# Two graph layers on sparse lists: variances and score sums on ScalarE, Newton steps and column copies in another iteration, five pair sums in a tile

## The chip, the cores and the metric

The kernel runs on one core of one Trainium2 chip. The metric is device time in microseconds (us) of one execution. The kernel before took 1013.26 us (median of three runs, 1010.72 to 1016.06); the execution that was profiled took 1008.23 us, of which its trace spans 1006.5 us.

In the text PE or TensorE is the matmul engine, DVE is VectorE, ACT is ScalarE, POOL is GpSimd and SP is SyncE, which here only issues transfers.

## The reference, cut to what matters

A graph of N = 3327 nodes with 512 features each passes through two layers, each with a residual and a layer norm. The adjacency matrix has a handful of ones in a row.

```python
# layer 0: graph attention with 4 heads of 128
feats  = einsum('nf,hfo->hno', x, W)
logits = leaky_relu(e_s[:, :, None] + e_n[:, None, :], 0.2) + NEG_INF * (1 - adj)
out    = relu(softmax(logits) @ feats + b)            # heads side by side: 512
x      = layernorm(x + out)
# layer 1: one attention over neighbours and one plain sum, each with a gate
attn_a = sigmoid([adj @ x, x] @ Wa.T + ba)
attn_b = sigmoid([adj @ x, x] @ Wb.T + bb)
h      = x @ W_sa
e      = where(adj != 0, exp(-leaky_relu(s_left[:, None] + s_right[None, :], 0.01)), 0)
x_a    = (e / (e.sum(1) + 1e-5)) @ h
x_b    = adj @ (x @ W_gcnb) + b_gcnb
x      = layernorm(x + sigmoid(attn_a * x_a + attn_b * x_b))
```

The layer norm is (y - mean) / sqrt(variance + 1e-5) over the 512 features.

## The kernel before, in words

The function `sparse_pass` does the work in three stages. Nodes lie in 26 tiles of 128. Every engine runs its own instructions in the order in which the program gives them (a manual schedule); engines wait for each other by semaphores.

**Preparation.** The adjacency matrix comes in seven chunks of 512 columns, through 12 buffers. For each chunk TensorE turns it into codes (`make_codes`), VectorE takes from them the list of each node's neighbours (`top_codes`, `decode`, `pick`). Between the chunks `features` computes one tile of layer 0's features after another on TensorE (L346), ScalarE copies them into a row (L350 to L352), and GpSimd writes the rows to `table0` in DRAM (L353). Behind the last tile one more small write, of `nrow` (L355), sets the scores of the padding row to -1e30. Nodes are sorted by their number of neighbours, in two groups of 12 and 14 tiles: `rank_a`, `rank_b` and `sort` write the lists of group 0 in the order of rank during chunk 4 and those of group 1 after the last chunk. `own_x` then gathers group 0's own rows of x. The first tile of each group (tiles 0 and 12) has nodes with more neighbours than a tile has slots; the rest are in an extra row of gathers, the stairs. `climb(g)` moves the numbers and scores of these from the sorted list onto the right partitions, with one matmul (L538) and small copies of VectorE. `climb(0)` runs in the loop over chunks, at chunk 4 (`i == NC0 + 1`, with NC0 = 3).

**Layer 0.** The tiles come in an order of their own, `order0` (11, 10, 0 to 9, 12 to 25), and have as many rows to sum as neighbours: 16 for tile 0, down to 5 for tile 25. In iteration i, GpSimd issues the gathers for tile i + 3 (L602, one instruction a row of 128 x 520 floats, into seven buffers of six rows), and:

- `weigh_a` and `weigh_b` compute the softmax weights of tile i + 1: scores (L696), their maximum, Exp on ScalarE (L709), sum, reciprocal and product (L714 to L716);
- `attend` multiplies every gathered row by its weight, two thirds of the rows on VectorE (L733), every third on ScalarE (L731), and TensorE adds them up in PSUM by matmuls with the identity (L736), behind one for the bias (L725);
- for tile i - 1, VectorE adds x (L810, `scalar_tensor_tensor`, called STT in places), and `columns1` transposes the result on TensorE (`x1t`, L753); `stats` takes mean and variance with bn_stats (L647, L648);
- for tile i - 2, `columns2` copies the transposed tile to SBUF on ScalarE (`xt`, L757) and multiplies it with eight vectors (`pcol`, L760), from which layer 1 gets its scores and gates; `columns3` copies these (L764).

Variances are gathered in groups of up to four tiles (`Norm`). At the end of a group, `rsqrt` computes 1/sqrt with an integer start and three Newton steps on VectorE (L656 to L663, 13 small instructions), and two iterations later `publish` scales the group's tiles (ScalarE, L768), corrects the eight columns (VectorE, L771 and L772) and scatters each tile's rows to `table1` (GpSimd, L143).

**Layer 1** starts when all rows of `table1` are written. Tiles come in `order`: six short ones, then long and short in turn, last three of 9, 9 and 7 rows. In iteration i:

- `weights_a` and `weights_b` compute the attention weights and gates of tile i + 1: a copy on ScalarE (L861), the sums of scores on VectorE, one for each gather buffer (L863), leaky ReLU (L870), Exp on ScalarE with an accumulated sum (L872), gates (L874 to L887), L892 to L895;
- `scaled_first` starts the weighted sum `sw` on ScalarE (L914), and `weighted` adds the rows to it on VectorE, one STT each (L930);
- the plain sum of the same rows is made by TensorE, one matmul with the identity a row (L951). To spare matmuls, VectorE adds some rows two and two (L932): `paired` chooses up to four pairs in a tile, five where there are 13 rows or more. Part 0 of `weighted` goes up to the last pair, part 1 is what is left;
- `turn` and `project` transpose both sums and multiply them with two matrices of 512 x 512 (L961, L963, L970), for tile i - 1;
- for tile i - 2 follow the gated sum (L995), Tanh on ScalarE (L997), the residual (L1018), bn_stats and, at the end of a group, the Newton steps; an iteration later ScalarE scales the group (L1011) and GpSimd scatters it to the output.

Of the kernel before, what the change touches and what calls it, by code (L numbers as in the profile page):

```python
# [14 lines left out]
P = 128  # L15
# [64 lines left out]
def sparse_pass(  # L80
# [213 lines left out]
    nrow = pj.tile([1, ROW], F32, name="nrow")  # L294
    nc.gpsimd.memset(nrow, 0.0)
    nc.gpsimd.memset(nrow[:, F : F + H], -BIG)
# [42 lines left out]
    def features(t):  # L339
# [11 lines left out]
        nc.scalar.copy(row[:, F:ROW].rearrange("p (h o) -> p h o", h=2), pf[:, :, F // 2 : HC])  # L351
        nc.scalar.copy(st[:, t, S + 2 : S + 2 + H].bitcast(F32), pf[:, 1, F // 2 : HC])  # L352
        nc.gpsimd.dma_start(table0[t * P : (t + 1) * P, :], row)  # L353
        if t == NT - 1:
            nc.gpsimd.dma_start(table0[N:NP, F : F + H], nrow[:, F : F + H])  # L355
# [194 lines left out]
    for i in range(len(chunks)):  # L550
# [11 lines left out]
        if i == NC0 + 1:  # L562
            climb(0, p0, psl.tile([P, CH], F32, tag="pc1", name="climb0")[:, : B + H])
# [3 lines left out]
    nc.sync.dma_start(own1[:, 1, :], table0[NG[0] * P : NP, :])  # L567
    rank_a(1)
# [76 lines left out]
    def stats(pool, y, mv):  # L645
        st6 = pool.tile([P, 6], F32, tag="st6", name=f"st6_{nc.next_id()}")
        nc.vector.bn_stats(st6, y)  # L647
        nc.vector.bn_aggr(mv, st6)  # L648

    def rsqrt(pool, mv, n, tag):  # L650

        v = pool.tile([P, GRP], F32, tag="rv", name=f"rv{tag}")[:, :n]
        r = pool.tile([P, GRP], F32, tag="rr", name=f"rr{tag}")[:, :n]
        t = pool.tile([P, GRP], F32, tag="rt", name=f"rt{tag}")[:, :n]
        d = pool.tile([P, GRP], F32, tag="rd", name=f"rd{tag}")[:, :n]
        nc.vector.tensor_scalar(v, mv[:, :n, 1], LN_EPS, None, ALU.add)  # L656
        nc.vector.tensor_scalar(t.bitcast(I32), v.bitcast(I32), 1, None, ALU.logical_shift_right)
        nc.vector.tensor_scalar(r.bitcast(I32), t.bitcast(I32), -1.0, float(0x5F3759DF), ALU.mult, ALU.add)
        for _ in range(3):
            nc.vector.tensor_mul(t, r, r)  # L660
            nc.vector.scalar_tensor_tensor(t, t, -0.5, v, ALU.mult, ALU.mult)
            nc.vector.scalar_tensor_tensor(r, t, 1.5, r, ALU.add, ALU.mult)
        nc.vector.scalar_tensor_tensor(d, mv[:, :n, 0], -1.0, r, ALU.mult, ALU.mult)  # L663
        return r, d

    class Norm:


        def __init__(self, pool, tag, ends):
            self.pool, self.tag, self.ends = pool, tag, ends  # L670
            self.first, self.mv = 0, None

        def add(self, k, y):

            if self.mv is None:
                self.mv = self.pool.tile([P, GRP, 2], F32, tag="mv", name=f"mv{self.tag}{k}")
            stats(self.pool, y, self.mv[:, k - self.first, :])
            if k not in self.ends:
                return None
            n = k - self.first + 1  # L680
            done = (self.first, *rsqrt(self.pool, self.mv, n, f"{self.tag}{k}"))
            self.first, self.mv = k + 1, None
            return done
# [70 lines left out]

    def columns2(j):
        xt1 = m0.tile([P, KT, P], F32, tag="xt1", name=f"xt1_{j}")
        nc.scalar.copy(xt1, turned[j])  # L757
# [36 lines left out]
    ready = [[], []]  # L794
    for i in range(NT + 3):
# [3 lines left out]
        for args in ready[0]:  # L799
            publish(*args)  # L800
        ready = [ready[1], []]
        if 2 <= i < NT + 2:
            columns2(order0[i - 2])
        if i < NT:
            attend(order0[i])
        if 0 < i <= NT:
# [3 lines left out]
            nc.vector.scalar_tensor_tensor(y, accs[j], 0.0, xj, ALU.max, ALU.add)  # L810
            columns1(j)
            done = norm.add(i - 1, y)
            if done:
                k0, scale, shift = done
                ready[1] = [
                    (order0[k], scale[:, k - k0 : k - k0 + 1], shift[:, k - k0 : k - k0 + 1]) for k in range(k0, i)
                ]
        if 2 <= i < NT + 2:
            columns3(order0[i - 2])
# [656 lines left out]
```

## Time and profile before

| | PE | DVE | ACT | POOL |
|---|---|---|---|---|
| busy, us of the 1006.5 us span | 798.0 | 719.3 | 270.5 | 635.8 |
| share of the span | 79% | 71% | 27% | 63% |

The shares are means over stages with different limits, so they name no bound by themselves. By stretches of 50 us, TensorE, VectorE and GpSimd are busy as follows (us of 50):

| stretch | PE | DVE | ACT | POOL | granted PE clock |
|---|---|---|---|---|---|
| 100 to 150 (preparation) | 44.28 | 42.78 | 10.67 | 17.92 | 1.00 |
| 150 to 200 (preparation) | 19.89 | 30.23 | 3.75 | 16.77 | 0.63 |
| 400 to 450 (layer 0) | 44.27 | 32.87 | 19.93 | 38.42 | 0.85 |
| 550 to 600 (between the layers) | 37.08 | 34.74 | 15.29 | 27.24 | 0.86 |
| 850 to 900 (layer 1) | 45.86 | 45.14 | 13.45 | 39.03 | 1.00 |

A gather occupies GpSimd for 0.95 us or more and is followed by 0.3 us that are not counted as busy, so 38 to 39 us of 50 is GpSimd without a break. In a row of the waits, the engine and line before the arrow stood idle until the one behind it was done; then come the total in us, the number of times and the longest. In a timeline the columns are the start in us, the time taken, engine, line, operation, written and read tiles with their shape and the number of instructions, and in brackets the idle time before them with what ended it.

### The profile page before, as it was taken

Reading aid. Unit: us, or ns where it says so; the run is one execution under the profiler, and the core shown is the slowest. Engines: PE = TensorE matmul, PEld = TensorE weight load, DVE = VectorE, ACT = ScalarE, POOL = GpSimd, SP = SyncE. Lnnn points to the kernel's source line nnn. Section 1 sums busy time; section 2 is a strip of 40 time slices with the busy share of each in tenths; the row PEclk is TensorE's granted clock in tenths of the full one; section 3 lists DMA queues with packets and bytes.
Section 4 is the critical chain, followed back from the end, with each engine's and each line's share of the span. In section 5 each row is a group of like instructions: output and inputs, shape, how many; then the busy total and the mean of one; then the engine's idle time right before and its main releaser. Section 6 shows DMA issues by size and latency. Waiting matters only on the chain.

```text
span 1006.5 us, 9964 instructions
## 1 busy us (share of the span) xinstructions
PE 798.0 (79%) x2534; PEld 422.2 (42%) x2534; DVE 719.3 (71%) x2131; ACT 270.5 (27%) x737; POOL 635.8 (63%) x677
## 2 busy tenths in 40 slices
PE   4398982518797996989698949998998989898991
PEld 3277762204344443444344424444444434343440
DVE  4277896586366673856566848897987989899882
ACT  1021210103134242333424413323221232321331
POOL 6611151577777777777777647777777777777211
PEclk9699995657889998889899968999999999999996
DMA  8799995995877777777777537776776667767200
GB/s 321 291 356 400 367 388 197 322 372 200 269 206 206 219 207 225 209 232 229 218 237 230 178 118 199 192 193 197 192 194 194 177 185 189 199 184 190 72 32 34
DMA packets 71954, 221.86 MB, mean 220 GB/s; under 512 B 13425, under 2 KB 17697, under 8 KB 70993
## 3 DMA queue, kind: packets, MB, share of 16 engines
q0 software_dynamic: 48000, 157.07, 52.7%
q1 hardware_dynamic: 22784, 61.97, 16.3%
q10 hardware_dynamic: 1104, 2.10, 0.6%
q8 instruction: 23, 0.38, 0.1%
q14 instruction: 43, 0.34, 0.1%
HBM read 200.01 MB, written 28.54 MB: 227 GB/s over the span
## 4 chain that ended last, share of the span: by engine, by line
PE 31%; DMA 17%; POOL 17%; DVE 16%; issue 13%; ACT 4%; DVEq 0%; POOLq 0%; ACTq 0%
POOL g L602 12%; PE acc L736 12%; DMA g<-table,srt 12%; PE pf L346 8%; DVE sw L930 6%; PE po L970 3%; DVE g L932 2%; PE pcol L760 2%; DMA at<-in_adjB 2%; PE acc L725 2%; PE acc L951 2%; ACT za L1011 1%; POOL out L143 1%; DMA a_row<-in_a_self 1%; POOL sprod L316 1%
## 5 line engine op out<-in xcount | busy, mean ns | idle before, releaser
L602 POOL DMA_INDIRECT g<-table,srt x464 | 477.2, 1028 | 145.8 <-issue 126.0
L736 PE MATMUL acc<-g,ident 128*128 128x512 f32 x504 | 232.5, 618 | 1.5 <-DVE g L733 1.5
L930 DVE SCALAR_TENSOR_TENSOR sw<-g,e,sw 128x512 f32<-128x512 f32 x226 | 169.3, 749 | 15.8 <-ACT sw L914 11.7
L736 PEld LDWEIGHTS acc<-g,ident 128*128 128x128 f32 x504 | 101.2, 201 | 133.6 <-issue 105.9
L951 PE MATMUL acc<-g,ident 128*128 128x512 f32 x262 | 124.9, 606 | 19.7 <-DVE g L932 19.6
L346 PE MATMUL pf<-w,xc 128*128 128x260 f32 x416 | 100.1, 402 | 13.8 <-DVE w L289 13.8
L733 DVE TENSOR_TENSOR g<-g,w 128x512 f32<-128x512 f32 x176 | 110.5, 695 | 0.6
L970 PE MATMUL po<-wsa,sT 128*128 128x512 f32 x208 | 95.6, 603 | 0.2 <-ACT sT L963 0.2
L346 PEld LDWEIGHTS pf<-w,xc 128*128 128x128 f32 x416 | 82.5, 201 | 28.6 <-DVE w L289 14.3
L970 PE MATMUL po<-wg,sT 128*128 128x512 f32 x208 | 93.5, 593 | 0.0
L731 ACT ACTIVATE g<-g,w 128x128 f32<-128x128 f32 x304 | 91.6, 390 | 2.7 <-DVE w L716 2.7
L951 PEld LDWEIGHTS acc<-g,ident 128*128 128x128 f32 x262 | 49.1, 192 | 88.4 <-issue 44.2
L353 POOL DMA_DIRECT2D table<-row x26 | 14.4, 554 | 95.2 <-ACT st L352 81.2
L932 DVE TENSOR_TENSOR g<-g 128x512 f32<-128x512 f32 x95 | 65.7, 691 | 3.3
L696 DVE TENSOR_TENSOR w<-g,srt 128x20 f32<-128x20 f32 (+3 forms) x55 | 9.7, 180 | 80.7 <-DMA g<-table,srt 79.7
L760 PE MATMUL pcol<-v,xt 128*128 128x8 f32 x208 | 33.2, 287 | 40.5 <-ACT xt L757 40.5
L143 POOL DMA_INDIRECT out<-za,srt x26 | 28.3, 1090 | 54.7 <-ACT za L1011 48.6
L970 PEld LDWEIGHTS po<-wsa,sT 128*128 128x128 f32 x208 | 40.6, 195 | 51.7 <-issue 49.5
L997 ACT ACTIVATE za<-za 128x512 f32<-128x512 f32 x26 | 16.4, 632 | 167.0 <-DVE za L995 167.0
L970 PEld LDWEIGHTS po<-wg,sT 128*128 128x128 f32 x208 | 39.6, 190 | 49.7 <-issue 49.2
L709 ACT ACTIVATE w<-w 128x40 f32<-128x40 f32 (+10 forms) x26 | 6.2, 237 | 176.8 <-DVE w L708 176.8
L760 PEld LDWEIGHTS pcol<-v,xt 128*128 128x128 f32 x208 | 30.9, 228 | 46.0 <-ACT xt L757 46.0
(234 smaller groups left out, 954.5 us busy)
## 6 DMA issues: line engine op xcount, KB each, us to landing
at<-in_adjB SPq DMA_DIRECT2D x78, 512.0 KB, 11.7
g<-table,srt POOLq DMA_INDIRECT x464, 3.8
table<-row POOLq DMA_DIRECT2D x26, 260.0 KB, 5.8
xc<-in_xB SPq DMA_DIRECT2D x6, 1024.0 KB, 7.4
own<-in_xo SPq DMA_DIRECT2D x1, 3640.0 KB, 31.2
own<-table SPq DMA_DIRECT2D x1, 3640.0 KB, 49.6
at<-in_adjL SPq DMA_DIRECT2D x13, 256.0 KB, 7.3
w<-in_W0B SPq DMA_DIRECT2D x1, 1040.0 KB, 6.9
```

The lines of the kernel that those rows point to most:

```text
L143: put = nc.gpsimd.indirect_dma_start(out=dst, out_offset=bass.IndirectOffsetOnAxis(ap=rows, axis=0), in_=src, in_offset=None, bounds_check ...
L346: nc.tensor.matmul(pf[:, hh, :HC], xc[:, k, o : o + P], w0[:, k, hh, :], start=(k == 0), stop=(k == KT - 1))
L602: nc.gpsimd.indirect_dma_start(out=buf[:, q - q0, :], out_offset=None, in_=table[:, :], in_offset=bass.IndirectOffsetOnAxis(ap=srt[g][:, i ...
L725: nc.tensor.matmul(acc, ident, bias0, start=True, stop=False)
L731: nc.scalar.activation(gv[:, h, :], gv[:, h, :], AF.Copy, scale=w[:, s, h : h + 1])
L733: nc.vector.tensor_tensor(gv, gv, w[:, s, :].rearrange("p (h o) -> p h o", o=1).to_broadcast([P, H, FO]), ALU.mult)
L736: nc.tensor.matmul(acc, ident, buf[:, o + s - s0, 0:F], start=False, stop=(s == CAPS[j] and j not in T0))
L760: nc.tensor.matmul(pcol, xt1[:, k, :], v1[:, k, :], start=(k == 0), stop=(k == KT - 1))
L930: nc.vector.scalar_tensor_tensor(sw, g[:, i, 0:F], e[:, s : s + 1], sw, ALU.mult, ALU.add)
L932: nc.vector.tensor_add(g[:, i, 0:F], g[:, i - 1, 0:F], g[:, i, 0:F])
L951: nc.tensor.matmul(plain[j], to, row, start=(not sums_of_two and i == 0), stop=(sums_of_two and i == len(rows) - 1),)
L970: nc.tensor.matmul(proj[j], sT[:, k, :], wt[:, k, :], start=(half + k == 0), stop=(half + k == KT))
```

## The change

- **Variances.** bn_stats and bn_aggr of VectorE go. The residual STT of both layers writes the sum of its row with its accumulator (`norm.total`), VectorE turns it into minus the mean, and ScalarE sums the squares of y - mean (`AF.Square` with a bias and an accumulator).
- **Newton steps.** They are called by `norm.finish` one iteration after the last variance of a group: in layer 0 behind the products of `attend` and ahead of the next residual, in layer 1 behind L995. The tiles are published in the same iterations as before.
- **Columns.** In layer 0 the copy `xt` is issued in `columns1`, right behind the transposes; the matmuls of `columns2` go behind `attend`, and `columns3` goes to the start of the next iteration.
- **Sums of scores.** L863 becomes an activation of ScalarE with the node's own score as its bias.
- **Pairs.** Up to five pairs in a tile, three in each of the last three tiles.
- **Preparation.** `climb(0)` goes behind the loop over chunks. The write of `nrow` goes: the copy of the last tile's scores adds a bias `pad`, -1e30 on the last partition and zero elsewhere.

The diff, cut:

```diff
@@ features
-        nc.scalar.copy(row[:, F:ROW].rearrange("p (h o) -> p h o", h=2), pf[:, :, F // 2 : HC])
+        nc.scalar.activation(
+            row[:, F:ROW].rearrange("p (h o) -> p h o", h=2), pf[:, :, F // 2 : HC], AF.Identity,
+            bias=pad if t == NT - 1 else 0.0,
+        )
...
-        if t == NT - 1:
-            nc.gpsimd.dma_start(table0[N:NP, F : F + H], nrow[:, F : F + H])
@@ the loop over chunks
-        if i == NC0 + 1:
-            climb(0, p0, psl.tile([P, CH], F32, tag="pc1", name="climb0")[:, : B + H])
         more(4)
...
+    climb(0, p0, psl.tile([P, CH], F32, tag="pc1", name="climb0")[:, : B + H])
     rank_a(1)
@@ Norm.add
-            stats(self.pool, y, self.mv[:, k - self.first, :])
+            nc.vector.tensor_scalar(less_mean, less_mean, -1.0 / F, None, ALU.mult)
+            nc.scalar.activation(square, y, AF.Square, bias=less_mean, accum_out=self.of[:, 1, i : i + 1])
@@ columns1, columns2
+        xt1s[j] = m0.tile([P, KT, P], F32, tag="xt1", name=f"xt1_{j}")
+        nc.scalar.copy(xt1s[j], pt)
...
-        nc.scalar.copy(xt1, turned[j])
@@ the loop of layer 0
-        for args in ready[0]:
+        if 3 <= i < NT + 3:
+            columns3(order0[i - 3])
+        for args in ready:
             publish(*args)
...
+        if i < NT:
+            attend(order0[i])
         if 2 <= i < NT + 2:
             columns2(order0[i - 2])
-        if i < NT:
-            attend(order0[i])
+        if full:
+            k0, scale, shift = norm.finish(i - 2)
...
-            nc.vector.scalar_tensor_tensor(y, accs[j], 0.0, xj, ALU.max, ALU.add)
+            nc.vector.scalar_tensor_tensor(y, accs[j], 0.0, xj, ALU.max, ALU.add, accum_out=norm.total(i - 1))
             columns1(j)
...
-        if 2 <= i < NT + 2:
-            columns3(order0[i - 2])
@@ weights_a, paired
-            nc.vector.tensor_scalar(e[:, s0 : s0 + n], g[:, :n, F], row1(j)[:, F + 3 : F + 4], None, ALU.add)
+            nc.scalar.activation(e[:, s0 : s0 + n], g[:, :n, F], AF.Identity, bias=s_left)
...
-        left = 4 + (CAPS[j] >= 13)
+        left = 5 if j not in order[-3:] else 3
@@ the loop of layer 1
             nc.scalar.activation(za, za, AF.Tanh, scale=0.5)
+        if full:
+            ready = norm.finish(i - 3)
         if jp is not None:
             project(jp, 0)
...
-            nc.vector.scalar_tensor_tensor(za, za, 0.5, row1(jpp)[:, 0:F], ALU.mult, ALU.add)
+            nc.vector.scalar_tensor_tensor(
+                za, za, 0.5, row1(jpp)[:, 0:F], ALU.mult, ALU.add, accum_out=norm.total(i - 2)
+            )
...
-            ready = norm.add(i - 2, zs[jpp])
+        full = jpp is not None and norm.add(i - 2, zs[jpp])
```

## The prediction

> **What bounds the kernel now.** I read the profile page first, then the busy time in stretches of 50 us, the waits (of GpSimd alone, then of all engines), and the timelines of single engines around the three places that the waits pointed to. The stretches give the stages: preparation to 197 us (first gather of layer 0), layer 0 until 593 us (first gather of layer 1), layer 1 until 1006.5 us.
>
> The waits of the whole span, cut to the ones that matter here (engine, line, what it waited for: total us, times, longest):
>
> ```profile
> ACT w L709 <- DVE w L708: 176.8, 25, 29.7
> ...
> ACT xt L757 <- PE x1t L753: 79.8, 19, 7.8
> DVE w L696 <- DMA g<-table,srt: 79.7, 22, 8.6
> ...
> PE pcol L760 <- ACT xt L757: 40.5, 24, 7.5
> ...
> PE climb L538 <- DVE of L537: 20.3, 1, 20.3
> ```
>
> *Preparation* holds one hole: TensorE stands 20.3 us at the matmul of `climb(0)`, because the in-order VectorE reaches `climb`'s copies only after the lists of chunk 4 (169.0 us). The timeline of TensorE shows what queues behind it:
>
> ```profile
> 148.10 0.95 PE L393 MATMUL pv<-ident,v 128*128 128x128 f32 x8
> 169.38 0.58 PE L538 MATMUL climb<-of,to_row 128*128 128x14 f32 x2 [20.32 <-DVE of L537]
> 169.79 8.89 PE L346 MATMUL pf<-w,xc 128*128 128x260 f32 x32
> ```
>
> The last two feature tiles (L346) come 20 us late; with them the last rows of the table and all gathers. GpSimd then loses 6 us more to the write of `nrow`, which waits for the row before it:
>
> ```profile
> 180.60 0.60 POOL L353 DMA_DIRECT2D table<-row  x1
> 187.31 0.57 POOL L355 DMA_DIRECT2D table<-nrow  x1 [6.11 <-DMA table<-row]
> ```
>
> *Layer 0.* From 188 to 569 us no idle stretch of GpSimd is longer than 0.31 us: a gather costs 0.95 + 0.30 us, and VectorE waits 79.7 us for gathered rows. So gather issue sets the pace, and the other engines have a little slack: TensorE is busy 306 of 362 us (230 to 592). How little, a boundary between two tiles on TensorE shows:
>
> ```profile
> 455.42 0.60 PE L753 MATMUL x1t<-ident,x1b 128*128 128x128 f32 x4
> 456.75 1.06 PE L760 MATMUL pcol<-v,xt 128*128 128x8 f32 x8 [0.73 <-ACT xt L757]
> 457.67 1.10 PE L725 MATMUL acc<-bias,ident 128*128 128x512 f32 x2
> 458.61 9.61 PE L736 MATMUL acc<-g,ident 128*128 128x512 f32 x22
> ```
>
> From the end of one tile's sums (455.42) to the next one's first row (458.61) it takes 3.2 us; a row is two passes of 0.43 us.
>
> *Layer 1.* VectorE waits for rows only once here (0.7 us between 605 and 935), while the last gather is issued at 932 us and VectorE still works until 975. So VectorE with its short waits is the bound, GpSimd runs ahead. What one tile's turn costs beside the row sums:
>
> ```profile
> 948.39 0.29 DVE L895 TENSOR_SCALAR e<-e,gate 128x10 f32<-128x10 f32 x1
> 948.59 0.68 DVE L647 BATCH_NORM_STATS2 st<-za 128x6 f32<-128x512 f32 x1
> 949.31 0.18 DVE L648 BATCH_NORM_AGGREGATE mvn<-st 128x2 f32<-128x6 f32 x1
> 949.47 1.54 DVE L930 SCALAR_TENSOR_TENSOR sw<-g,e,sw 128x512 f32<-128x512 f32 x2
> ```
>
> ```profile
> 948.71 0.72 ACT L914 ACTIVATE sw<-x1b,e 128x512 f32<-128x512 f32 x1 [0.99 <-DVE e L895]
> ```
>
> L930 needs `sw` from ScalarE, which ends at 949.43. The variance (L647, L648) ends at 949.49: it lies wholly in the shadow of `sw`.
>
> **What the skill says.** (1) TensorE: Matmul & The Clock Gate, "Architectural detail": the queues of ScalarE and VectorE are strictly first in, first out. The trace agrees: the copy `xt` of L757 stands behind the Exp of L709 (at 274.4 us, after 20.6 us of idle time, TensorE waiting 7.5 us for it). (2) Same page, "Part 1: The HAM clock gate": after an idle window of about 3.4 us TensorE drops to half clock. The trace is less kind: gaps of 2.06 us (at 747) and 2.51 us (at 245) were followed by matmuls of half speed, one of 2.41 us (at 547) was not. (3) ScalarE: Activation LUTs, "What ACT_TABLE_LOAD costs": an activation with one pointer operand takes 280 ns + 0.833 ns an element, 0.71 us for 512; L914 has 0.72. (4) VectorE: DVE Perf Modes, "Two Vector instructions with no wait between them": an operation that also writes its accumulator is two instructions. No VectorE operation of before shows it; ScalarE's read of an accumulator (L872) takes 0.19 us.
>
> **The change, part by part.**
>
> *Preparation.* `climb(0)` goes behind the loop. Features 24 and 25 then run at 149.1 to 158.0 us (8.9 us, as above). GpSimd has the list back at 159.7 (before's time) and issues 12 gathers of x and two table rows: about 16.5 us, so the first gather of layer 0 starts at 176.3 and not 197.05, 20.7 us sooner, of which 6.1 is `nrow`. Its replacement, the bias of `pad`, makes one small activation a pointer one (0.1 us). VectorE begins chunk 5 when it is done with chunk 4, at 169.0 to 170, not 186.9; `climb(0)` adds 1.7 us behind chunk 6. Its gather is the 30th in the queue (about 213), `climb(0)` ends at about 205: hidden. So VectorE's first sums come about 15.5 us sooner (row sums at 215, not 230.5).
>
> *Layer 0.* Gone from VectorE: 26 x (0.69 + 0.18) us of variance, not on the path. New on ScalarE: 26 Squares, each about 0.75 + 0.19 us. What matters is order. Before, ScalarE's order was Exp(i+1), then `xt`(i-1). Now it is `xt`(i-1), Square(i-1), Exp(i+1), and `xt`(i-1) waits for the transposes x1t(i-1), which TensorE does after the sums of tile i and pcol(i-2). Behind that Exp queue the weights (L714 to L716) and so every row of tile i+1. VectorE can no longer run a tile ahead. The boundary, from the end of the sums: pcol 0.92, x1t 0.60, to `xt` 0.09, `xt` 0.49, Square with its read 0.78, Exp 0.24, L714 to L716 0.72, the copy of L764 0.1, the first product 0.69, to TensorE 0.06: 4.7 us in place of 3.2. When publishing (every fourth tile) 4 x 0.45 us more of VectorE come between. The Newton steps (2.5 us) fit in the time in which TensorE finishes its rows.
>
> One tile of r rows thus costs 0.86r + 4.7 + 0.45 us, and gather issue 1.265r + 1.33 us. These meet at r = 9.4; the mean is 254 rows / 26 tiles = 9.8. Up to tile 12 (in order; the long tiles of group 0 and a tile of 16) gathers lead: the sums of tile 12 end at about 396 us, not 420.4 (20.7 us of start, and some 4 us because data no longer pass through `xt` and pcol to the sums). The last 13 tiles have 5 to 14 rows (120 in all): 13 x 4.7 + 120 x 0.86 + publishing 7 = 171 us; before took 582.9 - 420.4 = 162.5: 9 us lost. In each boundary TensorE idles about 2.4 us; by the gaps above I take 4 in 10 to bring a half clock for one window of 3.4 us, 1.7 us each: 13 x 0.7 = 9 us (bounds 0 and 22). So of 24 us, 6 are left at the end of layer 0. The tail from there to layer 1 (STT, Square for bn_stats, Newton, publishing) stays within 0.3 us.
>
> *Layer 1.* Variance out of VectorE: 0, since `sw` ends no sooner. Sums of scores on ScalarE: 0.35 us off VectorE, but they stand behind the Tanh of L997, so where no row lies between L995 and L870 (about 10 tiles) 0.2 us is lost, elsewhere up to 0.35 gained: together -1. Newton steps after L995: there they fill the wait for Tanh and scores, so 8 x 0.6 = -5. Five pairs: three tiles (11, 12, 11 rows) get a fifth, two of the last three lose one; 96 sums in place of 95, 0.7 us. Accumulator reads of VectorE: 26 x 0 to 0.19, I take 0.1: +2.6. Square delays `sp` (L987) by up to 0.9 us; TensorE has 26 of 370 us free and takes that. Sum: about -2.5.
>
> **Rivals.** *A, the forecast* (0.45): start -24 by tile 12, +18 in the rest of layer 0, -2.5 in layer 1: -8.5, so 1013.3 - 8.5 = 1005. *B, the boundary does not bite* (0.25): TensorE keeps its clock, -24 + 9 - 5 = -20 to -22: 991. For it: the gap of 2.41 us that did no harm; VectorE's many waits for data. *C, slower* (0.18): every boundary draws a half-clock window or two: 13 x 1.7 = 22 and more, so layer 0 ends 7 us late, and in layer 1 the reads (0.19) and the late `sp` cost 2: 1022. For it: the gaps of 2.06 and 2.51 us. Against: 22 us presume every window hit. *D* (0.12): the x gathers, chunk 6 and the table rows, now together at 160 to 180, share the DMA engines (0.97 busy from 100 to 150 us), and the start gains half: 1012.
>
> **How the numbers follow.** Predicted is A, 1005. B reaches 985 if the boundary costs nothing at all, C up to 1035 with two windows at each; 985 to 1023 leaves out about 2 in 10. Under 1008.2 lie B, two thirds of A and little of D: 0.58; over 1018.3 lie C and edges: 0.21; between: 0.21.
>
> **What would show it.** Right: no wait at L538 and the first gather of layer 0 near 176; in layer 0 the wait of `xt` for x1t followed at once by Square and Exp, TensorE's waits at pcol gone and waits of 2 to 2.5 us at the first row (on VectorE's product) in their place, VectorE's waits for data much smaller; first gather of layer 1 near 587. Wrong: if VectorE still waits some 80 us for data in layer 0, the boundary does not bind (B); if the granted clock there falls below 0.85, C; if layer 1 is shorter by over 10 us, I have misread the shadow of `sw`.

## The result, and the profile after

The changed kernel takes 1025.24 us (median of four runs, 1024.38 to 1027.91), before takes 1011.99 us (1009.79 to 1016.06) beside it: a ratio of 1.0131, 95% interval 1.0092 to 1.017. It is 1.3% slower; the forecast was 1005. The profiled executions (1027.91 and 1008.23 us) lie further apart than the medians, 19.3 us of span against 13.3, so the differences below are those of the two traces. Before's trace is 4 to 6 us shorter than the medians of before (1012 to 1014), so the table below shows about that much too little of what a kernel gains on it.

On four of the six later occasions (the ones of start_only, start_only_2, layer1_only_norms and layer1_only_norms_2) before took 1131 to 1151 us on its chip, and the traces show waits whose end the profile puts to nothing that it can name (`remote`: 43 in start_only, none in before and after), so from these chips, called stalled below, only ratios to before on the same chip are used.

The stages of the two traces, and of the four experiments on a chip without such waits, in us. "To tile 12" is from the first gather to the end of the sums of tile 12; the last three columns are from the first gather of layer 1 to the last row sum, from there to the end, and both together.

| kernel | first gather | to tile 12 | tiles 13 to 25 | between the layers | sums of layer 1 | end | layer 1 |
|---|---|---|---|---|---|---|---|
| before | 197.1 | 223.5 | 162.3 | 10.3 | 380.2 | 33.1 | 413.3 |
| after | 179.4 | 229.9 | 180.4 | 15.6 | 384.8 | 35.7 | 420.5 |
| columns_back_2 | 179.2 | 220.0 | 167.6 | 9.9 | 385.5 | 35.3 | 420.8 |
| exp_first_2 | 178.3 | 220.6 | 166.4 | 15.6 | 385.1 | 35.4 | 420.5 |
| bias_thrice_2 | 178.9 | 223.8 | 167.1 | 15.6 | 386.3 | 35.3 | 421.6 |
| square_layer0 | 181.0 | 222.9 | 165.1 | 10.0 | 379.9 | 32.9 | 412.8 |

So against before the start gives 17.7, and the four stretches behind it lose 6.4, 18.1, 5.3 and 7.2.

The waits of the changed kernel, the answer to the first list of the prediction (engine, line, what it waited for: total us, times, longest):

```profile
ACT xt L760 <- PE x1t L757: 217.6, 26, 13.3
...
DVE den L718 <- ACT w L713: 121.2, 26, 8.7
...
PE acc L740 <- DVE g L737: 52.7, 21, 4.1
...
DVE w L700 <- DMA g<-table,srt: 22.4, 8, 6.4
...
PE climb L542 <- DVE of L541: 13.4, 1, 13.4
```

Two of these rows in before:

```profile
DVE den L714 <- ACT w L709: 9.7, 26, 0.9
...
PE acc L736 <- DVE g L733: 1.5, 1, 1.5
```

The copy `xt` now waits for TensorE in every one of the 26 tiles. The sum of the weights (`den`) waited for the Exp in every tile in before too, but for 0.9 us at most; now that the Exp stands behind `xt`, these waits are 121.2 us in place of 9.7. TensorE in turn waits for the products of VectorE, 52.7 us in place of 1.5. VectorE's wait for gathered rows fell from 79.7 to 22.4: gathers no longer set the pace. The waits at `pcol` are all but gone (1.4 us, before 40.5).

*Preparation.* TensorE and GpSimd of the changed kernel (timeline):

```profile
153.02 7.20 PE L349 MATMUL pf<-w,xc 128*128 128x260 f32 x32
...
206.88 0.58 PE L542 MATMUL climb<-of,to_row 128*128 128x14 f32 x2 [13.42 <-DVE of L541]
```

```profile
162.91 1.01 POOL L500 DMA_INDIRECT x1a<-in_x,srt  x1 [6.44 <-DMA srt<-lists]
...
169.64 0.59 POOL L359 DMA_DIRECT2D table<-row  x1
...
179.35 0.95 POOL L605 DMA_INDIRECT g<-table,srt  x1 [0.30 <-issue]
```

The last feature tiles are done at 160.2 and not at 178.7; the wait of `climb(0)` now comes late, where it holds up nothing but the end of the lists. The gathers of x, which need the list, start at 162.91; in before they started at 159.96, and I had taken 159.7. This delay lies ahead of the moved `climb(0)`: the last of the scatters that write the list was issued at 149.56, in before at 146.47. Why, I don't know. From there on it went as forecast, and the first gather of layer 0 starts at 179.35 in place of 176.3.

*Layer 0.* One boundary on TensorE, ScalarE and VectorE (timelines of the same microseconds):

```profile
475.20 0.95 PE L768 MATMUL pcol<-v,xt 128*128 128x8 f32 x8
476.01 0.63 PE L757 MATMUL x1t<-ident,x1b 128*128 128x128 f32 x4
476.48 1.02 PE L729 MATMUL acc<-bias,ident 128*128 128x512 f32 x2
479.58 2.84 PE L740 MATMUL acc<-g,ident 128*128 128x512 f32 x6 [2.08 <-DVE g L737]
```

```profile
476.68 0.59 ACT L760 COPY xt<-x1t 128x512 f32<-128x512 f32 x1 [9.86 <-PE x1t L757]
477.17 0.72 ACT L668 ACTIVATE squaren<-x1b,ofn 128x512 bf16<-128x512 f32 x1
477.79 0.19 ACT L668 ACTIVATION_READ_ACCUMULATOR squaren<-x1b,ofn 128x1 f32 x1
477.88 0.22 ACT L713 ACTIVATE w<-w 128x40 f32<-128x40 f32 x1
```

```profile
478.14 0.22 DVE L718 TENSOR_REDUCE den<-w 128x4 f32<-128x40 f32 x1 [8.03 <-ACT w L713]
...
478.84 3.83 DVE L737 TENSOR_TENSOR g<-g,w 128x512 f32<-128x512 f32 x6
```

Each step of the forecast boundary is there, in its order: transposes, `xt`, Square and its read, Exp, `den`, product. From the end of the sums (475.2) to the next first row it takes 4.4 us, which is also the median of the 25 boundaries (before 3.2); I forecast 4.7. What I had sized too small is what happens to the rows behind it. Two groups of 18 passes in the timeline of TensorE:

```profile
339.22 7.99 PE L740 MATMUL acc<-g,ident 128*128 128x512 f32 x18 [2.06 <-DVE g L737]
...
351.42 9.69 PE L740 MATMUL acc<-g,ident 128*128 128x512 f32 x18 [2.06 <-DVE g L737]
```

The first runs at 0.43 us a pass, the second takes 1.7 us more after a gap of the same length. The granted clock tells them apart (stretch in us, its length, TensorE's busy time and instructions, granted clock, busy share of the DMA engines, GB/s):

```profile
335.56:338.97 3.41, 1.60 (x9) 1.00 0.60 174
338.97:342.39 3.42, 3.17 (x8) 1.00 0.66 195
...
349.21:352.63 3.42, 1.36 (x4) 1.00 0.75 214
352.63:356.05 3.42, 3.42 (x5) 0.50 0.68 196
```

The second group ran for 3.4 us at half clock. (What decides it stands in the last section.) Each of the 26 tiles of layer 0 has one row group; summed over them, what goes beyond 0.16 + 0.43 us a pass is 11.8 us in before (7 slow groups) and 32.9 us in the changed kernel (17 slow groups). The expectations below have 12.3 and 34.0 for these sums.

*Between the layers.* VectorE (timeline):

```profile
587.48 0.68 DVE L826 SCALAR_TENSOR_TENSOR x1b<-acc,g 128x512 f32<-128x512 f32 x1
588.09 0.08 DVE L826 DVE_READ_ACCUMULATOR x1b<-acc,g 128x1 f32 x1
...
592.34 0.15 DVE L677 TENSOR_SCALAR rvn<-ofn 128x1 f32<-128x1 f32 x1 [1.25 <-ACT squaren L668]
...
594.74 0.69 DVE L826 SCALAR_TENSOR_TENSOR x1b<-acc,g 128x512 f32<-128x512 f32 x1
```

The sums of tile 25, the last, end at 589.7, but its residual starts at 594.74. Ahead of it stand the Newton steps of tile 24, which wait for tile 24's Square. That stands behind tile 24's `xt`, which waits for transposes that TensorE does behind the sums of tile 25.

*Layer 1.* The turn of the same kind as the one shown of before:

```profile
962.53 0.29 DVE L905 TENSOR_SCALAR e<-e,gate 128x10 f32<-128x10 f32 x1
962.73 0.15 DVE L666 TENSOR_SCALAR ofn<-ofn 128x1 f32<-128x1 f32 x1
963.62 1.54 DVE L940 SCALAR_TENSOR_TENSOR sw<-g,e,sw 128x512 f32<-128x512 f32 x2 [0.73 <-ACT sw L924]
```

```profile
962.86 0.72 ACT L924 ACTIVATE sw<-x1b,e 128x512 f32<-128x512 f32 x1 [1.00 <-DVE e L905]
963.49 0.71 ACT L668 ACTIVATE squaren<-za,ofn 128x512 bf16<-128x512 f32 x1
964.10 0.19 ACT L668 ACTIVATION_READ_ACCUMULATOR squaren<-za,ofn 128x1 f32 x1
964.37 0.69 ACT L997 ACTIVATE sp<-acc,gate 128x512 f32<-128x512 f32 x1
```

bn_stats is gone from VectorE, and a wait for `sw` stands in its place, as forecast. On ScalarE the Square now stands ahead of `sp`.

### The profile page after: what moved, and what is told of

It is laid out like the page before. It is cut to its first block, busy times and chain, and to the rows that moved or that the text cites. A ratio compares the mean times of both kernels' runs of the same rounds, so it can differ in the third digit from the quotient of the medians.

```text
span 1025.8 us, 10146 instructions
## 1 busy us (share of the span) xinstructions
PE 817.9 (80%) x2532; PEld 425.9 (42%) x2532; DVE 674.6 (66%) x2083; ACT 318.1 (31%) x890; POOL 637.0 (62%) x676
## 4 chain that ended last, share of the span: by engine, by line
PE 41%; issue 17%; POOL 14%; DVE 12%; DMA 9%; ACT 5%; DVEq 0%; POOLq 0%; ACTq 0%
PE acc L740 18%; PE po L980 10%; PE acc L961 8%; POOL g L605 7%; DMA g<-table,srt 6%; DVE sw L940 4%; PE pt L971 2%; ACT squaren L668 2%; DVE g L942 2%; ACT za L1023 1%; PE pcol L768 1%; POOL table L359 1%; DMA table<-row 1%; DVE g L737 1%; DMA a_row<-in_a_self 1%
## 5 line engine op out<-in xcount | busy, mean ns | idle before, releaser
L740 PE MATMUL acc<-g,ident 128*128 128x512 f32 x504 | 253.7, 664 | 58.6 <-DVE g L737 52.7
L740 PEld LDWEIGHTS acc<-g,ident 128*128 128x128 f32 x504 | 104.8, 212 | 208.9 <-issue 97.7
L940 DVE SCALAR_TENSOR_TENSOR sw<-g,e,sw 128x512 f32<-128x512 f32 x226 | 169.3, 749 | 30.5 <-ACT sw L924 26.5
L961 PE MATMUL acc<-g,ident 128*128 128x512 f32 x260 | 123.6, 609 | 12.4 <-DVE g L942 12.3
L349 PE MATMUL pf<-w,xc 128*128 128x260 f32 x416 | 105.3, 417 | 13.4 <-DVE w L289 13.4
L349 PEld LDWEIGHTS pf<-w,xc 128*128 128x128 f32 x416 | 85.8, 209 | 30.4 <-DVE w L289 14.1
L718 DVE TENSOR_REDUCE den<-w 128x4 f32<-128x40 f32 (+10 forms) x26 | 5.9, 226 | 121.2 <-ACT w L713 121.2
L961 PEld LDWEIGHTS acc<-g,ident 128*128 128x128 f32 x260 | 50.7, 197 | 80.5 <-issue 49.3
L760 ACT COPY xt<-x1t 128x512 f32<-128x512 f32 x26 | 15.2, 585 | 217.6 <-PE x1t L757 217.6
L377 PE MATMUL pc<-at,pow 128*32 128x512 bf16 (+1 forms) x182 | 24.1, 436 | 31.5 <-DMA at<-in_adjB 17.4
L353 ACT COPY row<-pf 128x512 f32<-128x512 f32 x26 | 15.2, 585 | 99.8 <-issue 55.0
```

The source lines that it names most:

```text
L349: nc.tensor.matmul(pf[:, hh, :HC], xc[:, k, o : o + P], w0[:, k, hh, :], start=(k == 0), stop=(k == KT - 1))
L377: nc.tensor.matmul(pc[32 * c : 32 * c + 32, : nt * P], pow2[:, s, :], loaded[i, m], start=(s == 0), stop=(m + 1 not in ms or s == 3),)
L740: nc.tensor.matmul(acc, ident, buf[:, o + s - s0, 0:F], start=False, stop=(s == CAPS[j] and j not in T0))
L940: nc.vector.scalar_tensor_tensor(sw, g[:, i, 0:F], e[:, s : s + 1], sw, ALU.mult, ALU.add)
L961: nc.tensor.matmul(plain[j], to, row, start=(not sums_of_two and i == 0), stop=(sums_of_two and i == len(rows) - 1),)
```

## Experiments

**The parts, one by one.** `start_only` is before with the preparation of the change alone.

```diff
-        if i == NC0 + 1:
-            climb(0, ...)
         more(4)
...
+    climb(0, ...)
     rank_a(1)
```

(and `pad` for `nrow`.) `layer1_back` and `layer0_back` are the changed kernel with the whole loop of that layer as before. `columns_back` undoes only the order of the columns of layer 0:

```diff
-        xt1s[j] = m0.tile(...)          # columns1
-        nc.scalar.copy(xt1s[j], pt)
+        nc.scalar.copy(xt1, turned[j])  # columns2
@@ the loop of layer 0
-        if 3 <= i < NT + 3:
-            columns3(order0[i - 3])
+        if 2 <= i < NT + 2:
+            columns2(order0[i - 2])
         if i < NT:
             attend(order0[i])
-        if 2 <= i < NT + 2:
-            columns2(order0[i - 2])
...
             full = norm.add(i - 1, y)
+        if 2 <= i < NT + 2:
+            columns3(order0[i - 2])
```

> The kernel before with the part 'preparation' of the change alone: climb(0) behind the loop over chunks, and the bias pad in place of the write of nrow. Lockstep theory: the first gather comes near 179 us as in the changed kernel (before: 197), and since layer 0 of before is paced by the issue of gathers, nearly all of these 17.7 us stay to the end: first gather of layer 1 near 577, time about 996 (993 to 1001), against 1012 of before. Rival (the start gives nothing that lasts: the rows come only 12.4 us sooner in the changed kernel, because transfers of chunks 5 and 6, of x and of the table rows share the DMA engines, and the rest is lost on the way): 1003 to 1010.

> The changed kernel with layer 1 as it was before: bn_stats and Newton steps on VectorE in their old places, sums of scores on VectorE, four pairs. Theory: from the first gather of layer 1 to the end the changed kernel takes 420.5 us, before 413.3, and this is the work of layer 1's own edits, so the time falls by about 7, from 1025 to 1018. Rival (what layer 1 lost is a clock or transfer effect of what lies before it, and its own edits save the 2.5 us that I forecast): 1025 to 1028.

> The changed kernel with the loop of layer 0 as it was before (bn_stats, Newton steps, copies and columns in their old places); preparation and layer 1 as changed. Theory: layer 0 is gather-paced again and the start's gain lasts; layer 1 costs 7 more than before: 996 + 7 = 1003 (1000 to 1008). Rival (the gain of the start is lost in any case): 1012 to 1019.

> The changed kernel with only the columns of layer 0 put back: the copy xt and the matmuls pcol ahead of attend in the next iteration, columns3 at the end of the iteration. The squares on ScalarE and the later Newton steps stay. Theory: it is the order of the columns that ties VectorE's products of a tile to TensorE's end of the tile before, so it alone cost the 17.9 us between tiles 12 and 25 and more of the start: back to about 1003 (1000 to 1008), ScalarE's waits at L760 for the transposes no longer followed by the Exp, and VectorE's waits for gathered rows near the 80 us of before. Rival (the Square, 0.9 us between the residual and the Exp of every tile, and the Newton steps ahead of the residual, cost it): 1018 to 1023.

On this chip, a stalled one, before took 1130.8 us. Ratios to it: start_only 0.9933 (0.9895 to 0.9971), layer1_back 1.0124 (1.005 to 1.0197), layer0_back 1.0022 (0.9987 to 1.0057), columns_back 0.9943 (0.988 to 1.0006). Against the expectations (1012 us there is a ratio of 1) start_only and layer0_back lie where the rivals had them, only columns_back where the theory had it, and layer1_back reaches over both. The sizes are no measure of an undisturbed chip. The order says this much: layer1_back and start_only differ in the loop of layer 0 alone, and their intervals lie apart, so that loop makes the kernel slower; columns_back, with the columns of that loop undone, is back at start_only within the intervals.

> The same kernel as columns_back (the changed kernel with only the order of the columns of layer 0 put back), on another chip, since on the first one all kernels ran 12% longer. Lockstep theory: start -15, layer 0 and the stretch to layer 1 as in before, layer 1 +7: ratio to before 0.992 (0.988 to 0.996), layer 0 from first gather to the last sums about 386 us as in before, not 410. Rival (Squares ahead of the Exp and Newton steps ahead of the residual cost it): 1.007 to 1.013.

On another chip columns_back took 999.51 us where before took 1014.0: ratio 0.9862 (0.9839 to 0.9885), better than the theory's 0.992 and just outside its range (0.988 to 0.996), far from the rival's. The change of the columns alone thus costs 1.0131 - 0.9862 = 0.027, some 27 us (23 to 32 by the two intervals). The stages say where: layer 0 is back to 387.6 us (before 385.8, after 410.3), the stretch between the layers to 9.9. The waits of layer 0 are those of before:

```profile
DVE w L700 <- DMA g<-table,srt: 88.0, 24, 7.1
...
ACT xt L761 <- PE x1t L757: 80.6, 18, 8.2
...
PE pcol L764 <- ACT xt L761: 36.2, 24, 7.7
```

The rival, that the Square's 0.9 us ahead of the Exp or the Newton steps ahead of the residual cost it, falls: both are still there.

**Which link ties the engines.** `exp_first` is the changed kernel with `xt` and Square moved behind the next tile's Exp; the other half of the new order, `columns3` waiting for `pcol` at the start of VectorE's iteration, stays:

```diff
             columns1(j)
-            full = norm.add(i - 1, y)
...
         if i + 1 < NT:
             weigh_a(order0[i + 1])
             weigh_b(order0[i + 1])
+        if 0 < i <= NT:
+            columns_copy(order0[i - 1])     # the copy xt
+            full = norm.add(i - 1, y)
```

> The changed kernel with the copy xt and the Square issued behind the Exp of the next tile instead of ahead of it; pcol behind attend and columns3 at the start of the next iteration stay. Lockstep theory: the wait of the Exp for TensorE's end of the tile is the costly link. What remains is columns3's wait for pcol: from the end of the sums pcol 0.92, columns3 0.1, first product 0.69, 0.06 to TensorE: 1.8 us, less than TensorE's own pcol, transposes and bias (2.46). So layer 0 gets nearly all back: ratio to before about 0.993 (0.988 to 0.997; start -15, layer 1 +7, tail +2). Rival (columns3 holds VectorE back just as the Exp did, since any wait of VectorE for the current end of TensorE ties them): 1.007 to 1.013.

> The same kernel as exp_first (the changed kernel with the copy xt and the Square behind the Exp of the next tile, columns3 still at the start of the iteration), on another chip. Lockstep theory, the Exp's link alone: from the end of the sums to the next first row 2.2 to 2.5 us instead of 4.5, so layer 0 gets nearly all back; the stretch between the layers stays at 15.6 us: ratio to before 0.992 (0.988 to 0.997). Rival (columns3 ties VectorE to the end of TensorE's tile in the same way): 1.005 to 1.013.

The first run fell on a stalled chip: 1.0077 (0.9977 to 1.0177), which tells nothing. The second gave 1003.45 us, ratio 0.9915 (0.9888 to 0.9942), as the theory had it (0.992). A boundary on TensorE (timeline of exp_first_2):

```profile
446.02 0.95 PE L769 MATMUL pcol<-v,xt 128*128 128x8 f32 x8
446.83 0.63 PE L757 MATMUL x1t<-ident,x1b 128*128 128x128 f32 x4
447.30 1.02 PE L729 MATMUL acc<-bias,ident 128*128 128x512 f32 x2
448.16 9.85 PE L740 MATMUL acc<-g,ident 128*128 128x512 f32 x22
```

2.1 us in place of 4.4, without a gap; this is the median of the 25 boundaries (expected 2.2 to 2.5). VectorE waits 84.2 us for gathered rows, `den` 8.0 us for the Exp, and layer 0 takes 387.0 us: gathers set the pace again. So the link that matters is the Exp behind `xt` (and the Square that moved with it, which columns_back shows to be harmless by itself). `columns3` waits too (24.4 us in 12 waits), and layer 0 is no longer for it than in columns_back_2 (387.6). The stretch between the layers stays at 15.6, as expected, since `xt` is still ahead of the Square; it accounts for the 5 us by which exp_first_2 trails columns_back_2.

**Gap or clock.** `bias_thrice` leaves all waits in place and keeps TensorE busy in the gap:

```diff
-        nc.tensor.matmul(acc, ident, bias0, start=True, stop=False)
+        for _ in range(3):
+            nc.tensor.matmul(acc, ident, bias0, start=True, stop=(_ < 2))
```

> The changed kernel, only the bias matmul of every tile of layer 0 is issued three times, each starting the sum anew, so that the last one counts: TensorE is busy for 1.7 us of the 2.1 to 3.6 us in which it would wait for the first product. Theory that half the loss of layer 0 is clock: row groups of layer 0 take 34.0 us in the changed kernel beyond 0.16 + 0.43 us a pass, 12.3 in before; with the gaps filled this falls to about 12, and the time from 1.013 of before to 0.993 (0.990 to 1.000). Rival (the excess is waiting for data, or the gaps that are left still lower the clock; the extra matmuls lengthen the boundary): 1.010 to 1.025.

> The same kernel as bias_thrice (the changed kernel with every bias matmul of layer 0 issued three times, which keeps TensorE busy in the gap), on another chip. Theory that half the loss of layer 0 is half clock after the gaps: the excess of the row groups over 0.16 + 0.43 us a pass falls from 34 us to about 12 and the ratio to before from 1.013 to 0.995 (0.990 to 1.002). Rival (the excess is waiting for data, or the matmuls lengthen the boundary): 1.010 to 1.025, with an excess of 30 or more.

On a stalled chip: 1.0446 (1.038 to 1.0512), outside both expectations; the changed kernel itself was not run on that chip, so nothing follows from it. On an undisturbed one: 1011.37 us, ratio 0.9976 (0.9958 to 0.9993), against 1.0131 of the changed kernel. Its timeline:

```profile
463.38 0.95 PE L769 MATMUL pcol<-v,xt 128*128 128x8 f32 x8
...
464.66 2.74 PE L730 MATMUL acc<-bias,ident 128*128 128x512 f32 x6
467.77 8.85 PE L741 MATMUL acc<-g,ident 128*128 128x512 f32 x20 [0.36 <-DVE g L738]
```

The boundary is as long as in the changed kernel, 4.4 us (463.4 to 467.8); only the idle part shrank, from 2.08 to 0.36 us. The excess of the row groups falls from 32.9 to 8.2 us (4 slow groups in place of 17), the granted clock between 230 and 560 us rises from 0.91 to 0.97, and layer 0 falls from 410.3 to 390.9 us. So of the 24.5 us that layer 0 lost in the trace, about 19 were TensorE at half clock after gaps of 2 us, and about 5 the boundary itself. By the medians and ratios the repeated matmuls made the kernel faster by 14 to 16 us, so the 19 may be a few us too large.

**Layer 1.** `layer1_norms` is start_only with layer 1's variances and Newton steps as changed. `square_layer0` is columns_back with all of layer 1 as before; of the change it keeps the preparation and layer 0's Squares and late Newton steps. `layer1_only_norms`, `layer1_only_scores` and `layer1_only_pairs` put one edit each back into it, the last two being one line each:

```diff
-            nc.vector.tensor_scalar(e[:, s0 : s0 + n], g[:, :n, F], s_left, None, ALU.add)
+            nc.scalar.activation(e[:, s0 : s0 + n], g[:, :n, F], AF.Identity, bias=s_left)
```

```diff
-        left = 4 + (CAPS[j] >= 13)
+        left = 5 if j not in order[-3:] else 3
```

> The changed kernel with the columns of layer 0 put back and layer 1 as it was before: of the change remain the preparation and, in layer 0, the Squares on ScalarE and the later Newton steps. Theory: columns_back_2 takes 420.8 us from the first gather of layer 1 to the end, before 413.3; the edits of layer 1 are what costs these 7 us, so the ratio to before falls from 0.986 to 0.979 (0.976 to 0.982), about 992. Rival (layer 1 is slower for another reason, such as data that arrive in another rhythm): 0.984 to 0.988.

square_layer0 took 991.34 us, ratio 0.9788 (0.9761 to 0.9814), the theory's 0.979. It is 2.1% faster than before and the best of all kernels here. Layer 1 takes 412.8 us in it, and 420.5 to 421.6 in the four kernels with the new layer 1, whatever their layer 0: the edits of layer 1 themselves cost the 7 us. By the table its gain is the preparation: the first gather comes 16.1 us sooner, layer 0 takes 2.2 us more, and the rest differs by 0.3 us at most (14.7 us in all by the traces, 21 by the ratio).

> The same kernel as start_only (before with the preparation part alone), on another chip than the first group, where all kernels ran 12% longer and engines stood still for some 2 us between instructions that wait for nothing. Lockstep theory: ratio to before 0.984 (0.981 to 0.988), about 996 where before takes 1012. Rival (the start gives little that lasts, as the ratio of 0.993 there might say): 0.992 to 0.998.

> start_only with the variances of layer 1 as changed (sum by VectorE's accumulator, Square on ScalarE, Newton steps one iteration later behind L1005 of the changed kernel), but sums of scores and pairs as before. Theory: the Square ahead of the copy sp and the Newton steps ahead of the last residual are what layer 1 lost: it takes all of the 7 us, ratio to before 0.991 (0.988 to 0.994) where start_only has 0.984. Rival (the sums of scores behind the Tanh and the three pairs of the last tiles lost it): equal to start_only within 0.002, or 3 us faster.

> square_layer0 (0.979 of before; 412.8 us from the first gather of layer 1 to the end) with one edit of layer 1 put in: variances by VectorE's accumulator and ScalarE's Square, Newton steps an iteration later. Theory (the Square stands ahead of the copy sp, and at the end the Newton steps stand ahead of the last residual, and publishing ahead of the last Square): it carries most of the 7.5 us: 418 to 419, of which 2.5 after the last row sums; ratio to before 0.985 (0.983 to 0.987). Rival (the sums of scores carry the loss of the body; the norms only the 2.5 of the end): 415, ratio 0.981.

> square_layer0 with one edit of layer 1 put in: the sums of scores as activations of ScalarE. Theory that the norms carry most: +1.5, 414.3 us for layer 1, ratio 0.980 (0.979 to 0.982). Rival (they stand behind the Tanh on ScalarE, which waits for VectorE, so the leaky ReLU waits 12.5 us in place of 6.2 and all that follows with it): +5, 418 us, ratio 0.984.

> square_layer0 with one edit of layer 1 put in: up to five pairs in a tile, three in each of the last three. Theory: 0.5 to 1 us longer in all (one more sum on VectorE, 0.69; two of the last three tiles have one more row on TensorE, 0.86 each, where TensorE is the last to finish): 413.5, ratio 0.979 to 0.980. Rival (it gives back the rows that TensorE waits for elsewhere, or it carries the loss, since more pairs hold the matmuls behind VectorE): 410 or 416.

> The same kernel as start_only (before with the preparation part alone), on a chip without the stalls of the first two groups. Theory: the start alone gives the whole gain that the good kernels show (first gather 17.7 us sooner), and the Squares and late Newton steps of layer 0 give and cost nothing there since gathers pace it: ratio 0.980 (0.977 to 0.983), equal to square_layer0 within 0.003. Rival (the Squares relieve VectorE in layer 0 and give part of it): 0.984 to 0.988.

> The same kernel as layer1_only_norms (square_layer0 with the variances and Newton steps of layer 1 as changed), hoped for on a chip without the stalls. Theory (the norms carry most of what layer 1 lost): 418 to 419 us from the first gather of layer 1 to the end where square_layer0 has 412.8; ratio to before 0.985 (0.983 to 0.987). Rival (sums of scores or pairs carry it; the norms only the 2.5 us of the end): 415, ratio 0.981.

> The same kernel as start_only (before with the preparation part alone), hoped for on a chip without the stalls. Theory (gathers pace layer 0, so the Squares give nothing there): ratio 0.980 (0.977 to 0.983), equal to square_layer0's 0.979 within 0.003. Rival (Squares and late Newton steps give part of the gain): 0.984 to 0.988.

All of these fell on stalled chips, where an interval is 0.4 to 1% to either side. start_only gave 0.9845 (0.9766 to 0.9923), 0.9823 (0.9733 to 0.9914) and 0.9791 (0.9696 to 0.9887): a gain, equal to square_layer0's within the intervals, but the first group's 0.9933 is not, so whether the preparation alone gives all of it was not shown by times. layer1_norms gave 0.9883 (0.9812 to 0.9953). layer1_only_norms gave 0.995 (0.9904 to 0.9997) and, the second time, 0.9732 (0.965 to 0.9814); layer1_only_scores 0.9858 (0.9802 to 0.9914), layer1_only_pairs 0.9881 (0.9795 to 0.9966). The two answers on the norms contradict each other, and the other intervals reach over theory and rival, so which edit of layer 1 costs the 5 us of the row sums stays open. The end behind the row sums is settled, since the stalls leave it alone: it takes 35.3 to 35.7 us in all kernels with the new variances in layer 1 (35.4 in both runs of layer1_only_norms) and 32.9 to 33.2 in all without them (33.0 in layer1_only_scores and layer1_only_pairs).

What the traces show of it: TensorE's waits at the transposes for `sp` are 17.1 us (9) in the changed kernel, 8.7 (5) in before and 7.9 (6) in square_layer0. The largest, ScalarE and TensorE of the changed kernel (timelines):

```profile
947.68 2.91 ACT L1023 ACTIVATE za<-za,rdn,rrn 128x512 f32<-128x512 f32 x4
950.50 0.71 ACT L924 ACTIVATE sw<-x1b,e 128x512 f32<-128x512 f32 x1
951.11 0.71 ACT L668 ACTIVATE squaren<-za,ofn 128x512 bf16<-128x512 f32 x1
...
951.82 0.67 ACT L997 ACTIVATE sp<-acc,gate 128x512 f32<-128x512 f32 x1
```

```profile
952.54 0.66 PE L971 MATMUL pt<-ident,sp 128*128 128x128 f32 x4 [3.63 <-ACT sp L997]
953.03 1.56 PE L961 MATMUL acc<-x1b,ident 128*128 128x512 f32 x2
```

The same wait is 1.59 us in before. The two passes behind it take 1.56 us, not 1.02. From there to the last row sum at 990.1 TensorE does not stand once, so what delays it there delays the end; in before it stands another 2.0 us in this stretch, for pairs that VectorE has yet to add. The pairs have left a trace too: TensorE has 99 matmuls in this stretch, in before 95, since two of the last three tiles have three pairs and not four, and four passes are 1.7 us. And so have the sums of scores: the leaky ReLU of VectorE waits 12.5 us for them, in before 6.2 (one wait of 9.5 us for the first rows of the layer left out, which in before stands at L863). The traces don't say how the 5 us divide among the three. It is TensorE that ends the row sums: counted from the first gather of layer 1, VectorE's gated sum of the last tile but two comes 2.0 us earlier than in before (376.9, 378.9), the copy `sp` of the last tile 2.5 us later (384.9, 382.4).

The 2.6 us behind the last row sum are plain in VectorE's timeline:

```profile
1001.84 0.75 DVE L1005 SCALAR_TENSOR_TENSOR za<-bias_g,gate,po 128x512 f32<-128x512 f32 x1 [5.29 <-PE po L980]
1002.50 0.16 DVE L677 TENSOR_SCALAR rvn<-ofn 128x2 f32<-128x2 f32 x1
...
1004.94 0.69 DVE L1030 SCALAR_TENSOR_TENSOR za<-za,x1a 128x512 f32<-128x512 f32 x1
```

The Newton steps of the last but one group now stand ahead of the last residual; in before they ran while VectorE waited for TensorE (it still stood 1.97 us before the last gated sum).

## Why the prediction was wrong

The forecast was 8.5 us less, the traces have 19.3 more. Of these some 28 us, 10.4 lie in layer 0 up to tile 12, 9.7 in layer 1, 5.3 between the layers and 3.0 in the preparation. Step by step, in the order of the prediction:

- *Preparation, 20.7 us sooner:* right in mechanism, 17.7 measured. The term that was off is the return of the list, 3.2 us later than I took it, for a reason ahead of the edit. The rows come 12.4 us sooner (218.1), not 15.5; rival D, half the start lost, did not happen.
- *Layer 0 to tile 12, where "gathers lead" and 4 us are gained:* this step failed. The stretch lost 6.4 us. From the fourth tile on TensorE waits for products and not for gathered rows, with the same gaps of 2 us and more as later, and the half clock behind them (1.8 us in most slow groups) makes the tile longer than the 0.86r + 4.7 + 0.45 that I compared with the gathers. I had put the price of the clock at nothing for these tiles. bias_thrice_2, with the same boundary and the clock kept, takes 223.8 us there, as many as before (223.5); so the clock took some 6 of the 10.4 us, and with this boundary the gain of 4 does not come even then (columns_back_2, without it, has 3.5).
- *Tiles 13 to 25, 9 us for the boundary and 9 for the clock:* the sum was right by luck, 18.1 measured; the terms were not. With the clock kept, 4.8 us remain (167.1 against 162.3), so the clock took 13.3. A slow group costs what I had taken, but 7 of these 13 gaps brought one, not four in ten, and I counted them for 13 boundaries where there are 26. The four in ten did not follow from the three gaps that I had; it holds for the short gaps of these tiles (2.0 to 2.2 us, 4 of 9 slow), and those at publishing (3.2 to 3.8 us, 3 of 4) I had not set apart.
- *"The tail stays within 0.3 us":* failed, 5.3 us (15.6 in place of 10.3). I followed the chain from the last residual on, but not what stands ahead of it on VectorE. The experiments bear out the reading: the stretch is 15.6 us where `xt` is ahead of the Square (after, exp_first_2, bias_thrice_2) and 10 where it is not (columns_back_2, square_layer0, with the same late Newton steps in layer 0).
- *Layer 1, -2.5:* failed, +7.2. Right was the shadow of `sw`: taking the variance off VectorE brought nothing, its waits for `sw` rose from 11.7 to 26.5 us. Wrong was "VectorE with its short waits is the bound", and with it "TensorE has 26 of 370 us free and takes that" for the late `sp`, a term that I put at nothing: TensorE ends the row sums, and of its free time none is left from 952.5 us on. The Newton steps, which were to save 5 us, cost 2.6 at the end; what they did in the row sums can't be told from the other edits. How the 4.6 us of the row sums divide stays open.
- *The accumulator of VectorE, 0 to 0.19 us:* 0.08, shown above.

Of the rivals, C (slower, every boundary draws a half-clock window) named the mechanism that took most, and 1022 was near; but not every boundary draws a window (14 of the 22 gaps of 2 us and more did), and it put the loss into the last 13 tiles alone. B falls with the 79.7 us of waits for rows that became 22.4. The order of the new boundary, the gaps at the first row and the freed features were as written (at `climb` a wait of 13.4 us is left, where I had none, but it holds up no features). The granted clock in layer 0 did not fall below 0.85 as I had set for C (0.91 between 230 and 560 us, as in before). Such a mean is some 60 us at half clock in both (an estimate: twice 0.09 of 330 us). By the excess, twice 11.8 us of it lay in row groups in before and the rest in waits and other work; in the changed kernel it was nearly all. So the mean did not show the windows; the durations of the row groups did.

## What to carry to other kernels

Before a copy is moved ahead of another engine's input on an in-order queue, ask whose current work it waits for: a copy that waits for the end of TensorE's tile, put ahead of the Exp that feeds the next one, turned three engines that ran a tile apart into one chain. If TensorE must idle 2 us per tile, the price is the idle time plus the slow rows behind it; the durations of equal groups of matmuls show this, where the mean clock was 0.91 in before and after alike. Where a change has several parts, undo the one that alters an order first: here the place of one copy of 0.6 us (with the Square that goes with it) cost over 2%, more than the rest of the change gained.

## What the runs showed that I had not expected

- Two equal gaps of 2.06 us in TensorE's work were not equal: one brought half clock, the other did not. In the traces the granted clock changes only at steps of 3.41 us, and what counts is how long TensorE stands within one step (by the profile, which models the ends of matmuls). The slow group above had its gap whole in one step (busy 1.36 of 3.42 us, the next step at half clock); the other gap lay across the border of two (busy 1.60 of 3.41 us, and no change). In the six undisturbed traces, from 215 us to 30 us before the end, 74 of the 75 full-clock steps in which TensorE stood 2.0 us or longer were followed by one at half clock, and 7 of the 1066 in which it stood less. This sorts all 22 gaps of 2 us and more at the first rows of the changed kernel: the 14 with a slow group behind them have 2.04 us or more within one step, the other 8 at most 2.00. So what a gap just over 2 us costs depends on where it falls, and the 0.3 to 0.4 us that most gaps have left in bias_thrice_2 cost no clock wherever they fall. The Trainium skill (TensorE: Matmul & The Clock Gate, "Part 1: The HAM clock gate") speaks of an idle window of about 3.4 us; the length of the step agrees, but here 2.0 us of idleness in it were enough, and the measurement decides.
